# Two attention blocks in fp32 on one core: VectorE items between PSUM reads, the place of the first scores, and statistics on ScalarE

## The chip, the cores and the metric

The kernel runs on one core of a Trainium2 chip. The metric is the device time in microseconds of one execution; before the change it is 3248.27 us (median of 3 runs, 3246.43 to 3249.09). The profile is of one execution of its own, with a span of 3242.0 us, and all times inside the kernel below are microseconds from the start of that span.

A core has five engines that run side by side, each through its own list of instructions: TensorE (PE in the profile; its weight loads are PEld) multiplies matrices and writes to PSUM, VectorE (DVE) and ScalarE (ACT) work elementwise and read PSUM, GpSimd (POOL) and SyncE (SP) here mostly start transfers (DMA).

## The reference

Two attention blocks follow each other on an input of 8 images, 512 channels and 32 x 32 = 1024 positions. Both compute the same thing with weights of their own (biases and the affine part of the norm are applied too):

```python
def block(x):                                  # x: (8, 512, 1024)
    xg = x.reshape(8, 8, -1)                   # group norm, 8 groups of 64 channels
    xn = (xg - xg.mean(-1)) * rsqrt(xg.var(-1) + 1e-5)
    q, k, v = wq @ xn, wk @ xn, wv @ xn        # 512 x 512 each, 8 heads of 64
    p = softmax(q.T @ k * 64 ** -0.5, -1)      # per head, 1024 x 1024
    return x + wp @ (p @ v) + bias
return block1(block0(x))
```

All of it is fp32. The kernel works through 16 jobs, (image, block) pairs, two images in turn: (0, 0), (1, 0), (0, 1), (1, 1), (2, 0) and so on.

## The kernel before

Each job is a norm, three projections, an attention and an output projection. The projections use Strassen-like products: a 512 x 512 product becomes 7 products of halves; those for v stay at that level (the *v phase*), and those for the output (O), for k and for q are split once more into 7 *inner products* each. One stage of the kernel therefore does 21 *chains* of 7 inner products: O of the job before, then K and Q of the next. With the 64 steps of an attention a job has three stages:

- v phase, 7 products in two halves, while the output sums of the job before are formed
- the 21 chains (`deep_phases`; 14 in the first, where there is no O)
- attention: 8 groups (pair of heads, half of the positions) of 8 steps; a step makes scores on TensorE, their exp on ScalarE, a running sum on VectorE, and two steps later the value product on TensorE

A chain keeps its partial sums in four PSUM banks. Seven products go through three or four of them in the order 1, 5, 6, 2, 7, 3, 4, and each result is read by ScalarE (`copy`, `put(.., 0, ..)`) or by VectorE (`put(.., 1, ..)`, which adds `s5`):

```python
ORDER = (1, 5, 6, 2, 7, 3, 4)
def step(o):
    product(o, {1: z, 5: w, 6: z, 2: y, 7: z, 3: u, 4: z}[o], o in (1, 5))
    if o == 1:   nc.scalar.copy(y, z)
    elif o == 5: put5(w)             # ScalarE: s5 <- w
    elif o == 6: nc.scalar.copy(u, z)
    elif o == 2: put(0, 0, y)        # ScalarE
    elif o == 7: put(1, 1, z)        # VectorE reads z ...
    elif o == 3: put(0, 1, u)        # VectorE
    else:        put(1, 0, z)        # ... which o == 4 has written again; ScalarE
```

Two chains are interleaved, on the two halves of PSUM. VectorE has other work in this stage, which waits in three queues and is put into its instruction list just after its two PSUM reads in a chain: `soon` (sums that the next chains need: the `deep` sums of xn and the output sums of the chain after next), `outer` (the second level of the Strassen sums, 1024 elements each, and the additions to x) and `extra` (the statistics of the next norm, among others):

```python
def thunk(c, j):
    def go():
        if j == 0:
            live[c] = begin(c)           # may put four items into soon
        live[c](ORDER[j])
        if ORDER[j] in (7, 3):
            if soon:
                soon.popleft()()
            if outer:
                outer.popleft()()
            elif extra and extra[0][0] <= c:
                extra.popleft()[1]()
        if j == 6:
            end(c)                       # puts one to three items into outer
        ...
at = sorted((7 * c + 2 * j, c, j) for c in range(len(chains)) for j in range(7))
return [thunk(c, j) for _, c, j in at]
```

`begin` also forms the weight sums of the chain after next with four small VectorE additions (`factor`) where these weights are used for the first time: K and Q of block 0 ahead of the first attention, O of block 0 after it, K and Q of block 1 in the next stage, O of block 1 in the one after; later jobs load the finished sums. Four of the seven results of an output chain are added to x by an accumulating DMA on the GpSimd queue, started in `end`, and the others by VectorE.

At the end of the stage half 0 of PSUM is given to the scores while the last chain, on half 1, still has products to do; then half 1 is given to the value products:

```python
both = deep_phases(n + 1, extra, outs, ...)
both[0]()
rest[0]()
if n < 0:
    later(12.0, lambda: load_x(1))       # the second image, 2 MB
for thunk in both[1:-3]:
    thunk()
banks(0, "two")
att = Attention(n + 1)
att.scores(0)
att.scores(1)
for thunk in both[-3:]:
    thunk()
banks(1, "two")
```

`later(us, fn)` puts an instruction into its list after so many microseconds of a count of the products already listed; it waits for nothing at run time. The tile of the second image holds raw weights of q until they are stored, so that `load_x(1)` can start only after that.

The statistics of a norm are taken on VectorE, two half rows and an aggregation for each of four chunks of 128 channels. A gather through DRAM by two DMAs then brings them to eight partitions (`gather`), `groups` forms mean and variance, and `factors` and `apply` (ScalarE, four passes of 1024 elements) make xn:

```python
def stat(self, cc, sh):
    nc.vector.bn_stats(self.stats[:, cc, sh, :], xs[self.b][:, cc, sh * HALF : (sh + 1) * HALF])
    if sh == 1:
        nc.vector.bn_aggr(self.mv[:, cc, :], ...)
...
reads = [lambda cc=cc, sh=sh: norm.stat(cc, sh) for cc in range(NC) for sh in range(2)]
reads.append(norm.gather)
steps = [norm.groups, factors] + [lambda cc=cc: norm.apply(cc) for cc in range(NC)]
```

What is left of `extra` is put into the attention from step 2 on, one item a step, and `steps` and the sums of xn at fixed steps (10, 19, 22, 24, 26, 28, 36, 39, 42, 45). In the first attention the eight statistics of the second image come there, beside the weight sums of later jobs (`first_factors`), which the attentions of jobs 0 to 2 have.

Of the kernel before, what the change touches and what calls it, by code (L numbers as in the profile page):

```python
# [9 lines left out]
F32 = mybir.dt.float32  # L10
I32 = mybir.dt.int32
AF = mybir.ActivationFunctionType
ALU = mybir.AluOpType
# [5 lines left out]
P = 128  # L19
B, C, H, W = 8, 512, 32, 32  # L20
S = H * W
# [5 lines left out]
NC = C // P  # L27
# [43 lines left out]
def fast_path(  # L71
# [10 lines left out]
    nc = tc.nc  # L82
    xpool = ctx.enter_context(tc.tile_pool(name="xpool", bufs=2))
    acts = ctx.enter_context(tc.tile_pool(name="acts", bufs=1))
# [17 lines left out]
    xs = {}  # L102
# [3 lines left out]
    def later(delay, fn):  # L106
        todo.append((clock[0] + delay, fn))
# [34 lines left out]
    factors, deep = {}, {}  # L142
# [6 lines left out]
    def factor(w, part):  # L149

        if part == 0:
            nc.vector.tensor_add(w[:, S1], w[:, S3], w[:, A22])
        elif part == 1:
            nc.vector.tensor_sub(w[:, S2], w[:, S1], w[:, A11])
        elif part == 2:
            nc.vector.tensor_sub(w[:, S3], w[:, A11], w[:, S3])
        else:
            nc.vector.tensor_sub(w[:, S4], w[:, A12], w[:, S2])
# [53 lines left out]
    def load_x(b):  # L212
        for cc in range(NC):
            nc.sync.dma_start(xs[b][:, cc, :], x[b, cc * P : (cc + 1) * P, :])

    class Norm:
# [11 lines left out]
        def stat(self, cc, sh):  # L228
# [3 lines left out]
            if sh == 1:  # L232
                nc.vector.bn_aggr(
                    self.mv[:, cc, :], self.stats[:, cc, :, :].rearrange("p s k -> p (s k)")
                )

        def gather(self):

            dm = dram.tile([2, NC, HD, 2], F32, tag="dm", name=f"dm_{self.n}")
            for h in range(2):  # L240
                nc.sync.dma_start(
                    dm[h].rearrange("c p k -> p c k"), self.mv[h * HD : (h + 1) * HD]
                )
            self.gm = small.tile([GROUPS, HD, 2], F32, tag="gm", name=f"gm_{self.n}", bufs=1)
            nc.sync.dma_start(self.gm, dm.rearrange("h c p k -> (h c) p k"))
# [62 lines left out]
    def norm_steps(n):  # L308
        norm = Norm(n)

        def factors():
            norm.factors(slice(0, NC))
            xn[0] = acts.tile([P, NC, S], F32, tag="xn", name=f"xn_{n}")

        reads = [lambda cc=cc, sh=sh: norm.stat(cc, sh) for cc in range(NC) for sh in range(2)]
        reads.append(norm.gather)
        steps = [norm.groups, factors] + [lambda cc=cc: norm.apply(cc) for cc in range(NC)]
        return reads, steps

    xn, tx, to = [None], [None], [None]  # L320
# [182 lines left out]
    def deep_phases(n, extra, outs=None, early=()):  # L503
# [160 lines left out]
# [3 lines that stand above are left out]
                    live[c] = begin(c)  # L667
                live[c](ORDER[j])
                if ORDER[j] in (7, 3):
                    if soon:  # L670
                        soon.popleft()()
                    if outer:
                        outer.popleft()()
                    elif extra and extra[0][0] <= c:
                        extra.popleft()[1]()
                if j == 6:
                    end(c)
                    if c + 1 == len(chains):
                        while outer:
                            outer.popleft()()  # L680
                advance(0.43)

            return go
# [194 lines left out]
    def sums(n):  # L878


        def start():
            tx[0] = acts.tile([P, 3, 2, HALF], F32, tag="t", name=f"t_{n}")
            combine(xn[0], tx[0], 0)

        return [start] + [lambda part=part: combine(xn[0], tx[0], part) for part in (1, 2, 3)]
# [137 lines left out]
    def normed(chunks, cols):  # L1023
        for cc in chunks:
            norm.apply(cc, cols, cc % 2 == 1)
# [7 lines left out]
    var()  # L1033
    for i in range(3):
        idle_products(i % 2, "y", f"again_b{i}")
    for sh in range(2):
        norm.stat(2, sh)
    norm.factors(slice(0, 2))
    normed((0, 1), left)
    normed((0, 1), right_)  # L1040
    factor(v0, 0)
    for sh in range(2):
        norm.stat(3, sh)
# [46 lines left out]
    extra.append((6, load))  # L1090
    extra.extend((9, fn) for fn in bias_steps)
    reads, steps = norm_steps(1)
    extra.extend((10, fn) for fn in reads)
    for n in range(-1, len(jobs)):
        last = n + 1 == len(jobs)
        outs = None
        if n >= 0:
            chores = {}

            def put(i, fn):  # L1100
                while i in chores:
                    i += 1
                chores[i] = fn

            if last:
                w = plain_weights(n)
            else:
                if n == 0:
                    first_factors(put, [(O, 0), (V, 1)])
                elif n == 1:  # L1110
                    first_factors(put, [(K, 1), (Q, 1)])
                elif n == 2:
                    first_factors(put, [(O, 1)])
                for i, (_, fn) in enumerate(extra):
                    put(2 + i, fn)
                at = (10, 19, 22, 24, 26, 28, 36, 39, 42, 45)
                for i, fn in zip(at, steps + sums(n + 1)):
                    put(i, fn)
                deep_first = deep_steps(n + 1)
                for at, fn in zip((52, 54, 57, 59), deep_first[4:]):  # L1120
                    put(at, fn)
                put(61, lambda: (extend_plan(n + 1), [fetch() for _ in range(RING)]))
            assert max(chores, default=0) < NT * len(att.groups)
            att.run(chores)
            banks(0, "one")
            banks(1, "one")
            if last:
                advance(100.0)
                advance(100.0)
                judge()  # L1130
                plain_proj(n, w)
                break
            outs = OutputSums(n)
            out_sums(n, outs)
            first = v_phase(n + 1, ORDER)
            for thunk in first[:-1]:
                thunk()
            rest = first[-1:]
            extra = deque()
            if jobs[n][1] == 1 and jobs[n][0] + 2 < B:  # L1140
                extra.append((11, lambda b=jobs[n][0] + 2: (x_tile(b), load_x(b))))
            if n == 1:
                load, bias_steps = make_out_bias(1)
                extra.append((8, load))
                extra.extend((11, fn) for fn in bias_steps)
            if n + 2 < len(jobs):
                reads, steps = norm_steps(n + 2)
                extra.extend((15, fn) for fn in reads)
        both = deep_phases(n + 1, extra, outs, deep_first[:4] if outs else ())
        both[0]()  # L1150
        rest[0]()
        if n < 0:
            later(12.0, lambda: load_x(1))
        for thunk in both[1:-3]:
            thunk()
        banks(0, "two")
        att = Attention(n + 1)
        att.scores(0)
        att.scores(1)
        for thunk in both[-3:]:  # L1160
            thunk()
        banks(1, "two")

# [248 lines left out]
```

## Time and profile before

| | |
|---|---|
| time, median of 3 | 3248.27 us |
| span of the profile | 3242.0 us |
| TensorE busy | 3203.7 us |
| VectorE busy | 2771.0 us |
| ScalarE busy | 1896.9 us |
| mean DMA rate | 97 GB/s |
| granted clock of TensorE | 1.0 throughout |

The profile's first part gives each engine's busy time. The list of waits names for each engine and line what ended its idle time before an instruction, with the total, the number of times and the longest, in microseconds. The timeline lists instructions with start, duration, engine, line of the kernel, operation, output and input, and in brackets the idle time ahead of it and what ended it. An fp32 matmul of the inner products shows as two passes (x2); its duration includes the pipeline, so that the distance of two starts, not the duration, is what one costs. Matmul lines: L565 inner products, L434 products of the v phase, L736 scores, L767 values. PSUM reads by VectorE in the chains: L579 and L581; by ScalarE: L575, L577 and the copies at L381, L385 and L583. L594 are `outer` sums, L610 additions to x, L463 to L468 output sums, L366 to L372 `deep` sums, L152 to L158 weight sums, L229 and L233 statistics, L277 the applications of the norm, L753 the running sums of the attention and L783 their reduction.

### The profile page before, as it was taken

The page shows a single profiled execution, that of the slowest core. Times are in us where ns is not written, and L with a number is a line of the kernel's source. Part 1 is how long each engine was busy: PE and PEld are TensorE (multiplying, and loading weights), DVE is VectorE, ACT ScalarE, POOL GpSimd, SP SyncE. Part 2 cuts the span into 40 slices and gives each one's busy share as a digit, 9 for nine tenths or more (in the row PEclk, how much of TensorE's full clock was granted, in tenths as well). Part 3 has the DMA queues.
Part 4 walks back from the last instruction along what each step waited for, and adds up shares of the span by engine and source line. Part 5 has one row for each costly group of instructions (what it writes and reads, how often), then busy time and mean ns, then how long its engine had stood idle before and what let it go on. Part 6 is the DMA issues. An engine that isn't in the chain of part 4 may idle for free.

```text
span 3242.0 us, 57681 instructions
## 1 busy us (share of the span) xinstructions
PE 3203.7 (99%) x22870; PEld 1846.3 (57%) x22870; DVE 2771.0 (85%) x3968; ACT 1896.9 (59%) x3022; POOL 98.9 (3%) x93
## 2 busy tenths in 40 slices
PE   9999999999999999999999999999999999999999
PEld 7356384563836638366483654737547374573743
DVE  8997998979889797897978879788897888978876
ACT  4646646466564665656656565565656656566463
POOL 0000000000000000000000000000000000000000
PEclk9999999999999999999999999999999999999999
DMA  8234162350613305034160421505216051140501
GB/s 313 96 100 132 67 206 68 94 170 22 207 28 84 93 25 158 22 103 126 33 205 19 112 72 37 146 15 139 96 44 191 16 141 43 55 129 22 168 25 41
DMA packets 149462, 313.04 MB, mean 97 GB/s; under 512 B 33864, under 2 KB 46784, under 8 KB 148160
## 3 DMA queue, kind: packets, MB, share of 16 engines
q1 hardware_dynamic: 132320, 276.77, 26.0%
q0 software_dynamic: 16864, 32.51, 6.2%
q8 instruction: 181, 2.97, 0.4%
q14 instruction: 97, 0.79, 0.1%
HBM read 224.35 MB, written 51.18 MB: 85 GB/s over the span
## 4 chain that ended last, share of the span: by engine, by line
PE 89%; DVE 8%; DMA 1%; issue 1%; ACT 0%; DVEq 0%; SPq 0%
PE sc L736 26%; PE po L767 26%; PE vd L565 10%; PE zd L565 9%; PE z L434 6%; PE yd L565 4%; PE ud L565 3%; PE v L434 1%; PE u L434 1%; PE y L434 1%; DVE acc L753 1%; PE pp L705 1%; DVE p L581 1%; DVE x L610 1%; DVE p L594 1%
## 5 line engine op out<-in xcount | busy, mean ns | idle before, releaser
L741 ACT ACTIVATE e<-sc 128x1024 f32<-128x1024 f32 x1024 | 1046.8, 1024 | 584.9 <-PE sc L736 499.3
L736 PE MATMUL sc<-q,k 64*64 64x512 f32 x8192 | 1061.9, 590 | 2.0
L767 PE MATMUL po<-e,v 64*64 64x512 f32 x8192 | 1057.4, 589 | 0.0
L753 DVE TENSOR_TENSOR acc<-acc,e 128x1024 f32<-128x1024 f32 x768 | 935.9, 1219 | 54.8 <-ACT e L741 6.6
L767 PEld LDWEIGHTS po<-e,v 64*64 64x64 f32 x8192 | 313.2, 133 | 565.8 <-issue 556.7
L736 PEld LDWEIGHTS sc<-q,k 64*64 64x64 f32 x8192 | 310.0, 133 | 561.9 <-issue 545.7
L565 PE MATMUL vd<-deep,w 128*128 128x256 f32 x900 | 256.3, 383 | 5.1 <-DVE p L581 4.9
L565 PE MATMUL zd<-deep,w 128*128 128x256 f32 x892 | 248.1, 380 | 3.8 <-DVE p L579 3.2
L751 DVE TENSOR_TENSOR acc<-e,e 128x1024 f32<-128x1024 f32 x128 | 156.3, 1221 | 100.1 <-ACT e L741 100.1
L565 PEld LDWEIGHTS vd<-deep,w 128*128 128x128 f32 x900 | 167.9, 190 | 48.2 <-DVE p L581 13.0
L565 PEld LDWEIGHTS zd<-deep,w 128*128 128x128 f32 x892 | 169.0, 190 | 29.0 <-DVE p L579 5.1
L783 DVE TRANSPOSE_TENSOR_REDUCE r<-acc 128x32 f32<-128x1024 f32 x128 | 158.5, 1239 | 0.6
L565 PE MATMUL vd<-os,w 128*128 128x256 f32 x420 | 122.1, 384 | 14.5 <-DVE p L579 12.6
L608 POOL DMA_DIRECT2D x<-p x62 | 74.6, 1203 | 1996.8 <-ACT p L575 1521.9
L594 DVE TENSOR_TENSOR p<-p,p 128x1024 f32<-128x1024 f32 x94 | 114.2, 1215 | 0.0
L434 PE MATMUL z<-w,t 128*128 128x256 f32 x480 | 110.9, 379 | 0.0
L434 PE MATMUL z<-w,xn 128*128 128x256 f32 x480 | 110.1, 382 | 0.0
L385 ACT COPY ud<-vd 128x256 f32<-128x256 f32 x173 | 61.8, 357 | 77.2 <-PE vd L565 63.8
L583 ACT COPY s<-zd 128x256 f32<-128x256 f32 x173 | 64.5, 373 | 71.5 <-PE zd L565 71.5
L447 ACT COPY v<-z 128x512 f32<-128x512 f32 x32 | 18.8, 586 | 148.7 <-PE z L434 148.7
L434 PEld LDWEIGHTS z<-w,xn 128*128 128x128 f32 x480 | 90.0, 190 | 23.8 <-issue 12.2
L385 ACT COPY ud<-zd 128x256 f32<-128x256 f32 x156 | 55.7, 357 | 76.5 <-PE zd L565 74.6
(207 smaller groups left out, 4049.3 us busy)
## 6 DMA issues: line engine op xcount, KB each, us to landing
w<-deep SPq DMA_DIRECT2D x287, 448.0 KB, 3.9
w<-keep SPq DMA_DIRECT2D x129, 256.0 KB, 2.7
x<-p POOLq DMA_DIRECT2D x62, 512.0 KB, 6.9
rb<-rd SPq DMA_DIRECT2D x96, 256.0 KB, 4.0
deep<-w SPq DMA_DIRECT2D x42, 448.0 KB, 3.6
x<-x_dram SPq DMA_DIRECT2D x28, 512.0 KB, 6.4
out_dram<-x SPq DMA_DIRECT2D x28, 512.0 KB, 6.0
keep<-raw SPq DMA_DIRECT2D x5, 1792.0 KB, 7.7
```

Of the source, the lines that this page charges most:

```text
L385: nc.scalar.copy(u, z)
L434: nc.tensor.matmul(ps[:, ti * CH : (ti + 1) * CH], r[:, cc, t0 : t0 + P], w[:, cc, :], start=(start and ti == 0 and cc == 0), stop=(cc == ...
L565: nc.tensor.matmul(ps, lhs[:, FACTOR[i], :], moving[i], start=start, stop=True, skip_group_check=True,)
L583: return chain(product, lambda ps: nc.scalar.copy(s5, ps), put, z, y, u, w)
L594: outer.append(lambda: nc.vector.tensor_add(to_, a, b))
L608: nc.gpsimd.dma_start(to_, p(part), accum_op=ALU.add)
L736: nc.tensor.matmul(sc[h * HD : (h + 1) * HD, j, :], k[r, hp, k0 : k0 + HD], q[r, hp, sh * HALF : (sh + 1) * HALF], start=True, stop=True,)
L741: nc.scalar.activation(e, sc, AF.Exp, scale=SCALE)
L751: nc.vector.tensor_add(acc[g], self.es[i - 1], e)
L753: nc.vector.tensor_add(acc[g], acc[g], e)
L767: nc.tensor.matmul(po[g][j * HD : (j + 1) * HD, h, :], v[r, kc, d0 : d0 + HD], e[r, j, :], start=(kc == 0), stop=(kc == NT - 1),)
L783: nc.vector.tensor_reduce(self.r[:, 0, m, :], self.acc.pop(g).rearrange("p j (b e) -> p (j b) e", e=RP), AX.X, ALU.add, apply_transpose=True,)
```

## The change

It has five parts.

1. In a chain, one item at most goes onto VectorE's list after a PSUM read: an `outer` item only where no `soon` item was put.
2. The scores of the next attention are put two inner products from the end of q, no longer three.
3. The statistics of the second image (job 1) are taken by ScalarE in the first attention, as sums of x and then of (x - mean)^2 by the accumulator of an activation, whose elementwise output goes to the xn tile, which is free then. They no longer stand in `extra`; the later steps of that norm and the sums of xn move to later steps of the attention.
4. The load of the second image comes at 22 in place of 12.
5. At the start, the second half of one statistic of the first image moves behind the first applications of the norm.

Parts 1 and 2 are meant to keep VectorE's reads from standing behind other work while TensorE needs the bank, part 3 to take work off VectorE in an attention where it has the most, and part 4 to let weight loads go ahead of x.

```diff
+        def sums(self, cc):
+            nc.scalar.activation(
+                xn[0][:, cc, :], xs[self.b][:, cc, :], AF.Identity, accum_out=self.mv[:, cc, 0:1]
+            )
+        def less_mean(self):
+            nc.vector.tensor_scalar(self.off, self.mv[:, :, 0], -1.0 / S, None, ALU.mult)
+        def squares(self, cc):
+            nc.scalar.activation(
+                xn[0][:, cc, :], xs[self.b][:, cc, :], AF.Square, bias=self.off[:, cc : cc + 1],
+                accum_out=self.mv[:, cc, 1:2],
+            )
+        def by_count(self):
+            nc.vector.tensor_scalar(self.mv, self.mv, 1.0 / S, None, ALU.mult)
 ...  # norm_steps
+        if n == 1:
+            reads = [place] + [lambda cc=cc: norm.sums(cc) for cc in range(NC)]
+            reads.append(norm.less_mean)
+            reads += [lambda cc=cc: norm.squares(cc) for cc in range(NC)]
+            reads.append(lambda: (norm.by_count(), norm.gather()))
+            return reads, [norm.groups, factors] + [...]
 ...  # thunk of deep_phases
                     if soon:
                         soon.popleft()()
-                    if outer:
+                    elif outer:
                         outer.popleft()()
 ...  # start
-    for sh in range(2):
-        norm.stat(2, sh)
+    norm.stat(2, 0)
     norm.factors(slice(0, 2))
     normed((0, 1), left)
     normed((0, 1), right_)
+    norm.stat(2, 1)
 ...
     reads, steps = norm_steps(1)
-    extra.extend((10, fn) for fn in reads)
 ...  # ahead of each attention
                 at = (10, 19, 22, 24, 26, 28, 36, 39, 42, 45)
+                if n == 0:
+                    for i, fn in zip((3, 3, 4, 5, 6, 8, 10, 11, 12, 13, 15), reads):
+                        put(i, fn)
+                    at = (22, 30, 34, 35, 37, 38, 41, 44, 47, 50)
 ...
         if n < 0:
-            later(12.0, lambda: load_x(1))
-        for thunk in both[1:-3]:
+            later(22.0, lambda: load_x(1))
+        for thunk in both[1:-2]:
             thunk()
 ...
-        for thunk in both[-3:]:
+        for thunk in both[-2:]:
             thunk()
```

More of the change, by code (lines that the diff above doesn't have):

```diff
@@ L309, in norm_steps, with place @@
         norm = Norm(n)
+        def place():
+            xn[0] = acts.tile([P, NC, S], F32, tag="xn", name=f"xn_{n}")
         def factors():
             norm.factors(slice(0, NC))
-            xn[0] = acts.tile([P, NC, S], F32, tag="xn", name=f"xn_{n}")
+            if n > 1:
+                place()
+        if n == 1:
[3 more added lines that the diff above has]
+            reads.append(lambda: (norm.by_count(), norm.gather()))
+            return reads, [norm.groups, factors] + [lambda cc=cc: norm.apply(cc) for cc in range(NC)]
         reads = [lambda cc=cc, sh=sh: norm.stat(cc, sh) for cc in range(NC) for sh in range(2)]
```

## The prediction

> **What bounds the kernel now.** I read the shares of busy time first, then TensorE's waits, then the order of time around each wait.
>
> ```profile
> span 3242.0 us, 57681 instructions
> PE 3203.7 (99%) x22870; PEld 1846.3 (57%) x22870; DVE 2771.0 (85%) x3968; ACT 1896.9 (59%) x3022; POOL 98.9 (3%) x93
> ...
> PE vd L565 <- DVE p L579: 12.6, 15, 1.6
> PE vd L565 <- DVE p L581: 6.7, 22, 0.7
> PE zd L565 <- DVE p L579: 4.5, 4, 2.9
> PE v L434 <- DVE q L790: 2.5, 1, 2.5
> ...
> PEld sc L736 <- ACT p L577: 8.0, 15, 0.5
> ```
>
> The page says TensorE (PE) is busy for 99% and VectorE (DVE) for 85%: TensorE bounds the kernel, and no change that leaves its matmuls alone can gain more than its gaps. The waits (total us, times, longest) say where the gaps are: nearly all are matmuls of the inner products (L565) that wait for a VectorE read of the PSUM bank they are to overwrite (L579 and L581), once in each of the 15 later jobs at vd, and once at the scores. One wait of 2.5 us stands alone (L434), as does one of 2.9 us.
>
> The scores of successive jobs start, by the chain in order of time, at 83.59, 289.94, 495.90, 698.17 and 898.05 us and then every 199.88 us: the first three jobs take 206.35, 205.96 and 202.27 us, the other twelve 199.88. I laid the TensorE timeline of one such period against its own cadence (two passes of 128x256 in 0.43 us, a score or value step in 0.86) and got about 2 us that do no work, in two places. The first, from the timeline of all engines in job 3 after its start at 898 us:
>
> ```profile
> 1047.54 1.22 DVE L594 TENSOR_TENSOR p<-p,p 128x1024 f32<-128x1024 f32 x1
> ...
> 1049.40 0.41 DVE L468 TENSOR_TENSOR os<-to,os 128x256 f32<-128x256 f32 x1
> 1049.74 1.22 DVE L610 TENSOR_TENSOR x<-x,p 128x1024 f32<-128x1024 f32 x1
> 1050.03 0.59 PE L565 MATMUL vd<-os,w 128*128 128x256 f32 x2
> 1050.87 0.41 DVE L579 TENSOR_TENSOR p<-vd,s 128x256 f32<-128x256 f32 x1
> 1051.34 0.70 PE L565 MATMUL vd<-os,w 128*128 128x256 f32 x2 [0.71 <-DVE p L579]
> ```
>
> The columns are start, duration, engine, line, operation. Between two PSUM reads VectorE had both an item of `soon` (L467/L468) and one of `outer` (L610); so the read (L579) started at 1050.87, and the matmul that reuses the bank at 1051.34, where the cadence put it at 1050.46: 0.88 us lost. The second place, where the scores are put in:
>
> ```profile
> 1097.40 0.47 ACT L577 ACTIVATE p<-zd,bias_step 128x256 f32<-128x256 f32 x1
> 1097.93 1.95 PE L736 MATMUL sc<-q,k 64*64 64x512 f32 x16
> 1099.81 0.70 PE L565 MATMUL vd<-deep,w 128*128 128x256 f32 x2
> 1100.34 0.59 PE L565 MATMUL ud<-t,w 128*128 128x256 f32 x2
> 1100.61 0.48 DVE L581 SCALAR_TENSOR_TENSOR p<-vd,vec_sb,s 128x256 f32<-128x256 f32 x1 [1.80 <-PE vd L565]
> 1101.15 0.30 PEld L565 LDWEIGHTS vd<-deep,w 128*128 128x128 f32 x2 [0.61 <-DVE p L581]
> 1101.78 0.21 PEld L736 LDWEIGHTS sc<-q,k 64*64 64x64 f32 x8 [0.33 <-issue]
> ```
>
> The product before the scores ended at 1097.63; they waited 0.30 us for ScalarE to empty a bank of half 0. After them come the last three products: vd (o=7), ud (o=3), vd (o=4). The last overwrites what VectorE reads from the first, so it came at 1101.15 instead of 1100.77: 0.38 us. The remaining 0.45 us are the changes between 64-row and 128-row matmuls (0.15 and 0.20, and a slower first product), which stay.
>
> **What the Trainium skill says.** "PSUM — Partial Sum Buffer", section "Engine vs sequencer instructions", says that ScalarE, VectorE and GpSimdE queues are strict FIFO; the lines above agree: the 0.41 us read stood behind the 1.22 us addition. The same page, section "PSUM bank collisions raise a hardware error", wants semaphores by bank between a reader and TensorE, which is the wait here. "ScalarE: Activation LUTs", section "Table sets: the hidden batching unit", says that cheap functions are in every set and that a switch of sets costs a load; the profile shows one load (1283 ns) for Identity and Exp together, and the built program of the changed kernel also has one, so I take it that Square brings none. "DMA: Bandwidth & Descriptors", section "Issuing engines are not separate DMA queues", says that all transfers share 16 engines; in the first 90 us they are busy nearly throughout at a mean 292 GB/s, so a moved 2 MB load matters there.
>
> **The change part by part.** *One item per read (`elif`).* With one item of 1.13 us (its spacing in the run of adds) and two reads of 0.34 to 0.40 us, VectorE needs about 2 x (1.13 + 0.40) = 3.06 us for an inner chain of 7 x 0.43 = 3.02 us on TensorE: just even. With two items in a slot (0.77 + 1.13) it needs some 4.6 us in chain 3, which is the lag seen. After the change the `soon` items run in chains 0 to 3 and the six or seven `outer` items one by one in chains 5 to 8. I went through the order of the built program: the additions to x at L610 still stand ahead of the DMA accumulations to the same quarters (o=3 and o=4), so VectorE isn't made to wait for a DMA of 6.9 us. Gain: 12 jobs x 0.88 = 10.6 us; in jobs 0, 1 and 2 the corresponding gap is 1.33, 1.81 and 1.33, of which I give 4.0, since job 1 still has its weight sums between (0.93 us a chain). Together 14.6. Their earlier gaps (0.79 and 0.80 in jobs 0 and 2) come from the weight sums beside the `deep` sums and stay.
>
> *Two products from the end.* The o=7 product goes ahead of the scores: they start 0.43 us later than 1097.63, at 1098.06, when the bank (read until 1097.87) is free; and VectorE reads o=7 during the 1.72 us of scores. Gain 0.30 + 0.38 = 0.68 in 15 jobs and 0.38 in the first (no wait at 83.59): 10.6 us. The next step needs half 1 free: ScalarE would end its last read behind two exps at about 1101.6, and the value products come at about 1101.95, so I expect no new wait, by a margin of 0.3 us.
>
> *Statistics by ScalarE.* In the first attention VectorE loses 8 x 0.68 + 4 x 0.21 = 6.2 us and gets two small ones (0.3). It ends that attention behind: its last reduction (L783) starts at 201.99 where TensorE had done the last values at 195.87. That is the 2.5 us wait at L434 (2.71 with its restart) and some 0.35 at 227.87. The idle 3.59 us before the group statistics (they were asked for before their DMA had landed) also goes, as they stand at step 22. Gain 3.0. ScalarE takes on 8 passes from SBUF: an existing one (L277, 128x1024) takes 1.23 us, against an exp's 1.02. Four stand in successive steps: about 0.93 + 1.14 (each less the 0.09 by which two in a row overlap, as two exps take 1.94) and a read of the accumulator, an estimated 0.1 to 0.2, in a step of 1.716, so the lag grows 0.36 to 0.55 a step, 1.4 to 2.2 us in four; the score buffers allow some 1.3. I take 0.7 us off for this and the four applications in a row later. Net 2.3.
>
> *x load at 22 instead of 12.* At 67.35 a product waits 2.89 us (3.05 with restart) for VectorE, which waited for weights whose DMA was issued at 58.09, behind the 2 MB load of x, and landed after 7.82 us where the median of such loads in the first 90 us is 4.1. Now the load comes after three more weight loads; only the weights of the last chain are behind it. Gain 3.05 - 0.5 for those = 2.5.
>
> *Half a statistic moved at the start.* The first application starts some 0.5 us earlier, but TensorE then waits for the statistics of the last chunk all the same (pm at 14.50). 0.
>
> Sum: 14.6 + 10.6 + 2.3 + 2.5 + 0 = 30.0 us, or 0.9%; 3248.3 - 30.0 = 3218.3.
>
> **Rivals.** *VectorE becomes the bound*: the additions put off pile up in front of K's own and the statistics from chain 15. For it: 3.06 against 3.02 us. Against it: VectorE idles 0.4 to 1.7 us at nearly every read from 1059 to 1066, and has 13 us free of 61 in this stage. If true, half of 14.6 comes back: about 3226. *The scores' gaps return as a wait of the value products for half 1*: the margin is 0.3 us; it would give back up to 0.5 in each of 16, about 3226. *ScalarE's lag holds the scores up in the first attention*: four late buffers in place of one wait; up to 3 us, so part three nets nothing: 3221. *All is hidden behind TensorE*: not possible for these, as each gap is in TensorE's own timeline.
>
> **Range and chances.** The two large terms are counted from repeated gaps; each could be a quarter too large (6 us), the two small ones could be nothing (5 us). Little can make it better: jobs 0 to 2 have perhaps 4 us more. I set 3219.5, from 3213 to 3230. Over 2% would need 65 us, more than all gaps of TensorE together (38.3 us outside its busy time), so chance 0.01; over 2% slower needs a serious new wait, 0.01.
>
> **What would show it.** In the profile after, the wait of vd for L579's successor should fall from 12.6 to under 3 us, that of the scores for ScalarE from 8.0 to near the plain restart, and the period from 199.88 to about 198.3. The wait at L434 and the 2.89 us wait should be gone; ScalarE's busy time in the first attention should rise by some 10 us. A wait of x additions for a DMA, of value products for L577's successor or of scores for exps in the first attention would make me wrong.

## The result and the profile after

The changed kernel takes 3216.26 us (median of six runs, 3215.33 to 3217.55) where the kernel before takes 3247.69 (six runs beside them, 3246.43 to 3249.09). The ratio is 0.9904, with a 95% interval from 0.9891 to 0.9916. The span of the profile goes from 3242.0 to 3213.6 us, 28.4 less.

The medians thus differ by 31.4 us, 3 more than the profiles. The profile of before is of an execution of 3243.87 us, shorter than all six above, with a granted clock of 1.0 up to its last 2 us. The profiles of the first two runs below, which keep the long waits near 67 and 205 us (2.2 to 3.3 us), show TensorE at half clock just after them: for 6.8 and 3.4 us in one, for 3.4 and 3.4 in the other. The profiled execution of before has these waits without such a stretch. The changed kernel and its variants have no gap of 2 us or more, and no such stretch before their last 4 us. So some of the 3 us may come from these waits too; no run tests it.

In the changed kernel the lines of code stand lower: the inner products are L593 (before L565), VectorE's reads of them L607 and L609 (L579, L581), the scores L764 (L736), the products of the v phase L462 (L434), the additions to x L638 (L610), the running sums of the attention L779 and L781 (L751, L753) and their reduction L811 (L783). New are ScalarE's sums, L239, and squares, L247. The page begins like this, and TensorE's waits after it (total us, times, longest) answer to those shown of before:

```profile
span 3213.6 us, 57636 instructions
PE 3194.8 (99%) x22870; PEld 1850.2 (58%) x22870; DVE 2767.3 (86%) x3958; ACT 1902.4 (59%) x3038; POOL 99.4 (3%) x93
...
PE zd L593 <- DVE p L607: 3.3, 4, 1.4
PE vd L593 <- DVE p L609: 2.9, 6, 0.6
PE zd L593 <- DVE p L609: 1.9, 3, 0.9
PE pm L311 <- DVE mv L233: 1.8, 2, 1.2
...
PE v L462 <- DVE q L818: 1.3, 1, 1.3
...
PEld sc L764 <- ACT p L605: 5.2, 16, 0.3
```

The 12.6 us of vd on the first read are gone from the list, those on the second are 2.9 where they were 6.7, and the scores wait 16 times for 0.33 at most, the plain restart after ScalarE. What is left is in single places: the v phase (1.3, before 2.5) and a few waits of zd. The scores of successive jobs, by the chain in order of time:

| us | first scores | job 0 | job 1 | job 2 | jobs 3 to 14, each | last scores to end |
|---|---|---|---|---|---|---|
| before | 83.59 | 206.35 | 205.96 | 202.27 | 199.88 | 145.24 |
| after | 82.67 | 204.53 | 203.02 | 200.51 | 198.21 | 144.33 |
| difference | -0.92 | -1.82 | -2.94 | -1.76 | 12 x -1.67 = -20.0 | -0.91 |

The two places of a steady period that the prediction took apart look like this in the timeline of the changed kernel (start, duration, engine, line). First VectorE at the place where an item of `soon` and one of `outer` had stood together; the period starts at 888.94:

```profile
1037.84 0.41 DVE L495 TENSOR_TENSOR os<-to 128x256 f32<-128x256 f32 x1
...
1038.18 0.42 DVE L496 TENSOR_TENSOR os<-to,os 128x256 f32<-128x256 f32 x1
...
1039.28 0.42 DVE L607 TENSOR_TENSOR p<-vd,s 128x256 f32<-128x256 f32 x1 [0.68 <-PE vd L593]
...
1039.62 1.21 DVE L622 TENSOR_TENSOR p<-p,p 128x1024 f32<-128x1024 f32 x1
...
1039.94 1.03 PE L593 MATMUL vd<-os,w 128*128 128x256 f32 x4
```

Only the item of `soon` (L495 and L496) stands ahead of the read, so VectorE waits for TensorE there and no longer the reverse. The last line is two products in a row; the second writes the bank that the read at 1039.28 has emptied, with no idle time ahead of it. Then the scores, now with two products after them:

```profile
1086.56 0.59 PE L593 MATMUL vd<-deep,w 128*128 128x256 f32 x2
...
1087.08 1.95 PE L764 MATMUL sc<-q,k 64*64 64x512 f32 x16
...
1087.66 0.48 DVE L609 SCALAR_TENSOR_TENSOR p<-vd,vec_sb,s 128x256 f32<-128x256 f32 x1
...
1088.96 0.70 PE L593 MATMUL ud<-t,w 128*128 128x256 f32 x2
...
1089.50 0.59 PE L593 MATMUL vd<-deep,w 128*128 128x256 f32 x2
...
1090.13 0.47 ACT L605 ACTIVATE p<-vd,vec_sb 128x256 f32<-128x256 f32 x1
...
1090.93 1.04 PE L795 MATMUL po<-e,v 64*64 64x512 f32 x8
```

VectorE reads o=7 (1087.66) while the scores run, so the last vd comes 0.54 us after ud with nothing named ahead of it. ScalarE's last read of half 1 ends at 1090.60, and the value products come at 1090.93: the margin of 0.3 us that the prediction gave was there.

### The profile page after: what moved, and what is told of

The parts are those of the page before. It is cut to its first block, busy times and chain, and to the rows that moved or that the text cites. A ratio compares the mean times of both kernels' runs of the same rounds, so it can differ in the third digit from the quotient of the medians.

```text
span 3213.6 us, 57636 instructions
## 1 busy us (share of the span) xinstructions
PE 3194.8 (99%) x22870; PEld 1850.2 (58%) x22870; DVE 2767.3 (86%) x3958; ACT 1902.4 (59%) x3038; POOL 99.4 (3%) x93
## 4 chain that ended last, share of the span: by engine, by line
PE 93%; DVE 5%; DMA 1%; issue 1%; ACT 0%; SPq 0%; POOL 0%; DVEq 0%
PE sc L764 27%; PE po L795 26%; PE vd L593 10%; PE zd L593 10%; PE z L462 6%; PE ud L593 4%; PE yd L593 4%; PE v L462 2%; PE y L462 2%; PE u L462 2%; DVE acc L781 1%; PE pp L733 1%; DMA x<-p 0%; DMA w<-wqkv_dram 0%; DVE w L154 0%
## 5 line engine op out<-in xcount | busy, mean ns | idle before, releaser
L764 PE MATMUL sc<-q,k 64*64 64x512 f32 x8192 | 1061.7, 590 | 0.0
L781 DVE TENSOR_TENSOR acc<-acc,e 128x1024 f32<-128x1024 f32 x768 | 936.3, 1219 | 57.8 <-ACT e L769 9.3
L764 PEld LDWEIGHTS sc<-q,k 64*64 64x64 f32 x8192 | 309.7, 133 | 559.1 <-issue 545.4
L593 PE MATMUL vd<-deep,w 128*128 128x256 f32 x900 | 252.6, 380 | 1.4 <-DVE p L609 1.3
L779 DVE TENSOR_TENSOR acc<-e,e 128x1024 f32<-128x1024 f32 x128 | 156.4, 1222 | 111.3 <-ACT e L769 111.3
L593 PE MATMUL zd<-deep,w 128*128 128x256 f32 x892 | 248.4, 380 | 3.7 <-DVE p L607 2.0
L593 PEld LDWEIGHTS vd<-deep,w 128*128 128x128 f32 x900 | 170.6, 190 | 26.4 <-DVE p L609 2.5
L593 PEld LDWEIGHTS zd<-deep,w 128*128 128x128 f32 x892 | 168.9, 190 | 29.2 <-DVE p L607 3.3
L811 DVE TRANSPOSE_TENSOR_REDUCE r<-acc 128x32 f32<-128x1024 f32 x128 | 158.5, 1238 | 0.5
L593 PE MATMUL vd<-os,w 128*128 128x256 f32 x420 | 118.1, 380 | 1.6 <-DVE p L609 1.5
L462 PE MATMUL z<-w,t 128*128 128x256 f32 x480 | 110.9, 379 | 0.0
L462 PE MATMUL z<-w,xn 128*128 128x256 f32 x480 | 110.1, 382 | 0.0
L462 PEld LDWEIGHTS z<-w,xn 128*128 128x128 f32 x480 | 90.0, 190 | 23.8 <-issue 12.2
```

The source lines that it names most:

```text
L462: nc.tensor.matmul(ps[:, ti * CH : (ti + 1) * CH], r[:, cc, t0 : t0 + P], w[:, cc, :], start=(start and ti == 0 and cc == 0), stop=(cc == ...
L593: nc.tensor.matmul(ps, lhs[:, FACTOR[i], :], moving[i], start=start, stop=True, skip_group_check=True,)
L764: nc.tensor.matmul(sc[h * HD : (h + 1) * HD, j, :], k[r, hp, k0 : k0 + HD], q[r, hp, sh * HALF : (sh + 1) * HALF], start=True, stop=True,)
L779: nc.vector.tensor_add(acc[g], self.es[i - 1], e)
L781: nc.vector.tensor_add(acc[g], acc[g], e)
L811: nc.vector.tensor_reduce(self.r[:, 0, m, :], self.acc.pop(g).rearrange("p j (b e) -> p (j b) e", e=RP), AX.X, ALU.add, apply_transpose=True,)
```

## The experiments

In what the experiments expect, Theory 1 and Theory 2 are those that each text states. Where one time is given without a ratio, the kernel was executed once with its profile; what is concluded rests on places in the profile, not on the time.

### One item per read, alone

The kernel before, with part 1 only:

```diff
-                    if outer:
+                    elif outer:
```

> The kernel before with the one-item rule alone (an outer item only where no soon item was put). My account (a VectorE read that stood behind two items): in jobs 3 to 14 the period of the scores falls from 199.88 by 0.88 to 199.00 us, the 0.30 and 0.38 us gaps at the scores stay, and the wait of vd for the read at L579 (12.6 us) falls below 3 us; span about 3242 - 13 = 3229, ratio about 0.996. Rival (the work put off makes VectorE the bound later): the period falls by less than half of that and new waits for VectorE appear between chains 7 and 15.

Measured: 3233.5 us, ratio 0.9954 (0.9938 to 0.9971). The twelve steady periods are 198.90, which is 0.98 less each. Of TensorE's waits:

```profile
PE zd L565 <- DVE p L579: 6.7, 5, 3.3
PE vd L565 <- DVE p L581: 6.3, 22, 0.6
PE v L434 <- DVE q L790: 2.5, 1, 2.5
```

The line of vd on L579 (12.6) has gone, and the one on L581, which is the place of the scores, stays with its 22 times. So part 1 does what it was meant to, at 0.98 a job where 0.88 had been counted from one gap. The other tenth is in the product after the wait. In the kernel before it starts at 1051.34 and the next at

```profile
1051.87 0.59 PE L565 MATMUL yd<-q,w 128*128 128x256 f32 x2
```

which is 0.53 us later, where products otherwise follow in 0.43. The line of zd grew from 4.5 to 6.7; half of that is a wait in job 0 that went from 0.34 to 1.45 us (see "One addition of the first job on VectorE").

### The scores two products from the end, alone

The kernel before, with part 2 only:

```diff
-        for thunk in both[1:-3]:
+        for thunk in both[1:-2]:
 ...
-        for thunk in both[-3:]:
+        for thunk in both[-2:]:
```

> The kernel before with the first scores two inner products from the end instead of three, and nothing else. My account (the scores wait for ScalarE to empty half 0, the last product for VectorE's read of the third last): the period of jobs 3 to 14 falls by 0.68 to 0.8 us to about 199.1, the wait at 1050 of 0.71 us stays in every job; span about 3242 - 11 = 3231, ratio about 0.997. Rival (the gap moves to the value products, which then wait for half 1): a period of 199.4 or more and waits of the value products for ScalarE's read in each job.

Measured: 3237.28 us, ratio 0.9968 (0.9958 to 0.9979), steady periods 199.20, which is 0.68 less.

```profile
PE vd L565 <- DVE p L579: 12.6, 15, 1.6
...
PE vd L565 <- DVE p L581: 3.3, 6, 0.7
```

The mirror image: the wait on L579 stays whole, and the one on L581 loses 16 of its 22 times. 0.98 + 0.68 = 1.66, and both together gave 1.67. The two parts take away separate gaps, and neither gives back anything of the other.

### One product after the scores in place of two

```diff
-        for thunk in both[1:-2]:
+        for thunk in both[1:-1]:
 ...
-        for thunk in both[-2:]:
+        for thunk in both[-1:]:
```

> The changed kernel with the first scores one inner product from the end in place of two. My account of part two (three left: a wait for ScalarE's half 0 and one for VectorE's read; two left: neither; the margin of the value products against ScalarE's read of half 1 is about 0.3 us): with one left the scores still don't wait, but ScalarE's last read comes after both exps and the value products follow one product less after the scores, so they wait about 0.1 to 0.2 us: period of jobs 3 to 14 198.3 to 198.4 in place of 198.21. Rival (the further from the end the scores, the more is lost, as they only interrupt the products): the period falls below 198.15.

Measured: 3215.55 us, steady periods 198.21 as in the changed kernel. The small loss that was expected didn't come. One product or two after the scores makes no difference here; in both kernels the matmul of o=7 comes ahead of them.

### The second input's statistics back on VectorE

The changed kernel, with the statistics as VectorE items in `extra` again, but with the later steps (22, 30, 34 ...) of part 3 kept:

```diff
-        if n == 1:
+        if False:                       # the statistics by ScalarE are not used
 ...
+    extra.extend((10, fn) for fn in reads)
 ...
-                    for i, fn in zip((3, 3, 4, 5, 6, 8, 10, 11, 12, 13, 15), reads):
-                        put(i, fn)
```

> The changed kernel with the second image's statistics back on VectorE, but with the group statistics and what follows them at the later steps of the changed kernel. Theory 1 (in the first attention VectorE was late because it idled 3.59 us for the gather of the statistics; the later steps cure that, and the ScalarE passes cost VectorE 5.3 us of waiting for exps): VectorE idles under 2 us between steps 2 and 62, its last reduction starts 3 us or less after TensorE's last value product, against 4.3 in the changed kernel, and the wait of the v phase for VectorE (1.26 us) is gone; the first job's period falls from 204.52 to about 203.1. Theory 2 (taking 6.2 us of work off VectorE is what helped): the last reduction starts about 6 us late, the wait in the v phase is 2.5 us again, and the period is about 205.8.

Measured: 3216.28 us; the gap in the v phase is 0.80, smaller than the 1.42 of the changed kernel (1.20 in its second profile), and the first period is 203.49 in place of 204.53. Taking the statistics off VectorE gave nothing; the later steps alone give more. Why is seen in what VectorE waited for in the first attention (84 to 200 us), in the changed kernel:

```profile
DVE acc L781 <- ACT e L769: 2.9, 6, 0.8
DVE acc L779 <- ACT e L769: 2.4, 2, 1.6
DVE lt L842 <- DMA r<-r: 2.1, 1, 2.1
```

and in this one, with the statistics on VectorE:

```profile
DVE acc L778 <- ACT e L768: 1.0, 1, 1.0
DVE acc L780 <- DVE acc L780: 0.5, 1, 0.5
DVE acc L780 <- DVE acc L778: 0.5, 1, 0.5
```

ScalarE's eight passes stand between the exps, but delay them little: the ninth exp ends 16.35 us after the first scores where it is 15.42 with the statistics on VectorE, which is the largest delay, and from the seventeenth on they are level. VectorE, freed of the statistics, has nothing to do and waits for exps (5.3 us in all), and once for a transfer. Up to its last reduction it is busy for 102.07 us (106.53 before) and waits for 7.4 (3.6 before): most of what it was relieved of became idle time at a place where it keeps up with the exps. The kernel before had one such wait there, of 3.6 us for the transfer ahead of the group statistics, and the later steps remove it without help from ScalarE.

### ScalarE's passes spread out

The changed kernel with the passes at wider steps:

```diff
-                    for i, fn in zip((3, 3, 4, 5, 6, 8, 10, 11, 12, 13, 15), reads):
+                    for i, fn in zip((3, 3, 5, 7, 9, 11, 11, 13, 15, 17, 20), reads):
 ...
-                    at = (22, 30, 34, 35, 37, 38, 41, 44, 47, 50)
+                    at = (26, 32, 34, 35, 37, 38, 41, 44, 47, 50)
```

> The changed kernel with ScalarE's eight passes over the second image spread over steps 4 to 20 (at most two in a row) instead of 4 to 14, and the group statistics four steps later. Theory 1 (exps that come late behind passes in successive steps starve VectorE, which can't make up for it): VectorE's waits for exps in the first attention fall from 5.3 us to under 2.5, the wait for the gathered row sums of 2.1 us goes as its DMA is no longer behind the statistics', the last reduction starts 1 to 2 us after TensorE's last value product, and the v phase doesn't wait; first period about 203.1. Theory 2 (VectorE's lag comes from the work of the later steps, the sums of xn and the deep sums, alone): the last reduction starts some 4 us late as before and the period stays at 204.5.

Measured: 3217.24 us; gap in the v phase 1.95, first period 205.51. VectorE's waits for exps stayed at 5.2 us (the two lines of L779 and L781), and a wait of 2.1 us for a transfer (rb, at 132.65) took the place of the one at 122.77. The expectation of my own theory fell: spreading didn't take the waits away, which fits idle time better than late exps.

### VectorE's weight sums earlier

The changed kernel with the eight weight sums of the first attention at steps 9 to 22 in place of 12 to 33, so that they fill the idle time:

```diff
-                at += 3
+                at = next(places) if early else at + 3      # 9, 12, 15, 17, 19, 20, 21, 22
```

> The changed kernel with the eight weight sums of the first attention at steps 9 to 22 in place of 12 to 33, so that three of them leave the stretch after step 22; no work is added or taken away. Theory 1 (VectorE catches up and idles up to about step 19, 7.8 us in all, so work taken off it there is lost, and only what stands later counts): its waits in the first attention fall from 7.8 to about 4 to 5 us, the last reduction starts about 2 us less late (some 3 in place of 4.84 us after TensorE's last value product), the wait of the v phase for VectorE falls from 1.26 to 0 or nearly, and the first period from 204.53 to 203.1 to 203.5. Theory 2 (only the total of VectorE's work in the attention counts): the last reduction stays 4.8 us late and the first period at 204.5.

Measured: 3215.61 us; gap in the v phase 1.79, first period 205.15. The wait at 122.77 shrank to 0.3, as it should, but another took its place twelve microseconds later:

```profile
134.47 1.23 DVE L872 TENSOR_TENSOR q<-q,rb 128x1024 f32<-128x1024 f32 x1 [2.20 <-DMA rb<-rd]
```

So this expectation fell too: VectorE's idle time moved, and did not shrink.

### Half of the weight sums on GpSimd

Two more runs were to tell whether only VectorE's work after its last idle time counts. GpSimd does four of the eight weight sums, either the first four or the last four:

```diff
-                put(at, lambda i=i, part=part: factor(box[0][:, i], part))
+                put(at, lambda ...: factor(box[0][:, i], part,
+                    nc.gpsimd if <first attention> and i == 0 else None))    # the other run: i == 1
```

> The changed kernel with four of the eight weight sums that VectorE does beside the first attention (its steps 12 to 21, 0.68 us each, at 106.7 to 125.6 us, that is before or at VectorE's last idle time at 122.8) put on GpSimd. Theory 1 (what decides the wait at the layer's end is only the work that VectorE gets after its last idle time in the attention): these four take the place of idle time, so VectorE's idle time there grows by about 2 to 2.7 us, its last reduction still ends near 4.8 us behind TensorE's last value product, the wait of the value projection stays near 1.3 us and the period from the first scores to the second stays near 204.5. Theory 2 (the total of VectorE's work beside the attention decides): the reduction comes 2.7 us nearer to the value product, the wait falls below 0.5 us and the period to about 203.1. If GpSimd's sums slow VectorE's own instructions, it shows in the length of VectorE's additions of that stretch (0.4 to 1.2 us each before).

> The same with the other four sums (steps 24 to 33, at 129.4 to about 146 us, after VectorE's last idle time at 122.8). Theory 1: four times 0.68 = 2.7 us less lag at the end (about 2.1 us where it was 4.84), the wait of the value projection (1.3 us) all but gone, first period near 203.1; unless VectorE catches up in that stretch and finds a new wait, in which case its last idle time moves later and the lag falls by less than 2.7 by just that idle time. Theory 2: the same figures as with the early four, since the total is the same.

Measured: 3216.53 and 3214.21 us; first periods 203.94 and 202.85; gap in the v phase 0.46 in both. The pair doesn't tell the theories apart, as no step held GpSimd back: it did its sums between 92 and 103 us in both runs, and VectorE grew slow there. GpSimd and then VectorE in the run with the last four, from the timeline:

```profile
97.97 2.26 POOL L157 TENSOR_TENSOR raw<-raw 128x512 f32<-128x512 f32 x1
100.18 2.34 POOL L159 TENSOR_TENSOR raw<-raw 128x512 f32<-128x512 f32 x1
...
94.77 4.33 DVE L782 TENSOR_TENSOR acc<-acc,e 128x1024 f32<-128x1024 f32 x2 [0.44 <-ACT e L770]
99.02 1.24 DVE L245 TENSOR_SCALAR off<-mv 128x4 f32<-128x4 f32 x1
```

Two additions took 4.33 us, where two in a row otherwise take 2.54, and a four-element operation 1.24, which takes 0.17 in the changed kernel. The Trainium skill, "SBUF — State Buffer", section "Who interferes with whom", says that a VectorE instruction with two inputs in SBUF contends with a GpSimd instruction that reads SBUF, for a pair of ports that one of them holds exclusively. The additions agree with it: each grew by 0.9 us, beside GpSimd sums that took 1.27 us (the first) to 2.34. The four-element operation has one input, so that this sentence does not cover it; it grew by 1.07. So the pair took 2.7 us of work off VectorE and made its other work longer in an earlier stretch.

Against Theory 1, the early four helped as much as the late four. Against Theory 2, the lag did not fall by 2.7 us. What the pair does show is a floor. Let the lag be the time from TensorE's last value product, by its cadence, to the start of VectorE's last reduction:

| kernel | VectorE's last idle time in the first attention | lag | gap of TensorE in the v phase |
|---|---|---|---|
| before | 116.1 | 6.12 | 2.71 |
| passes spread out | 132.7 | 5.36 | 1.95 |
| weight sums earlier | 142.4 | 5.19 | 1.79 |
| changed kernel | 122.8 | 4.84 | 1.42 |
| changed kernel, second profile | 122.8 | 4.62 | 1.20 |
| statistics on VectorE, later steps | 167.9 | 4.21 | 0.80 |
| GpSimd, first four | 155.4 | 3.88 | 0.46 |
| GpSimd, last four | 154.5 | 3.87 | 0.46 |
| best (below) | 153.2 | 3.88 | 0.46 |

The gap is the lag less 3.41 in every row, to 0.01. So the wait follows from VectorE's lag alone in nine profiles. Where VectorE comes to wait for an exp once more at about 153 to 156, it has caught up, and the work placed after that leaves a lag of 3.9 (or 4.2). Where it does not, backlog remains at the end, and its size isn't told by the last idle time alone: the second to fourth rows are not in order.

### The start

The changed kernel with the old order of the first statistics (part 5 undone) and the second image's load still later:

```diff
-    norm.stat(2, 0)
+    for sh in range(2):
+        norm.stat(2, sh)
 ...
-    norm.stat(2, 1)
 ...
-            later(22.0, lambda: load_x(1))
+            later(27.0, lambda: load_x(1))
```

> The changed kernel with the statistics at the start in the old order and the second image's load at 27 in place of 22. My account: the old order takes 0.6 us off the start (the mean product of the last chunk waits 0.5 us for VectorE as before the change, not 1.20, and starts near 14.5), and with the weights of the last chain issued ahead of x the wait of 0.93 us (1.10 with restart) at 75.07 goes, so that the first scores come at about 81.0 us in place of 82.67, if the first loads of the input land alike. Rival for the load (x now comes too late for ScalarE's first sums, at step 4): the first scores still come at 81 to 81.5, but ScalarE waits for x at about 89 us and the first period grows by the wait. Rival for the start (the first landing of the input decides): no difference in the wait of the mean product.

Measured: 3213.95 us; first scores at 81.44, 1.23 earlier. In the changed kernel the weights of the last chain stand behind the 2 MB load of x (issued at 64.95 and 62.21), as the prediction had it, and VectorE waits for them:

```profile
73.60 0.29 DVE L152 TENSOR_TENSOR w<-w 128x128 f32<-128x128 f32 x1 [1.24 <-DMA w<-wqkv_dram]
...
75.07 0.70 PE L593 MATMUL zd<-deep,w 128*128 128x256 f32 x2 [0.93 <-DVE p L609]
```

With the load at 27 that gap of TensorE (1.10 us with its restart) is gone, and the later x holds nothing up. In nine profiles with the load at 22 the gap is 1.08 to 1.92, and in the two with it at 27 there is none. On part 5 the run gave no answer, since VectorE waited 0.37 us for the first weights. Over all runs, the gap of pm near 15 us is 1.28 to 1.39 in the nine profiles with the new order, and 0.76, 0.76, 0.98, 1.20 and 1.23 in the five with the old. The new order gains nothing and probably costs up to 0.6; how much isn't settled.

### One addition of the first job on VectorE

In job 0 the changed kernel has a gap of 1.53 us that was 0.49 before. Its cause by the timeline:

```profile
247.76 1.22 DVE L638 TENSOR_TENSOR x<-x,p 128x1024 f32<-128x1024 f32 x1 [2.25 <-DMA x<-p]
...
248.91 0.42 DVE L607 TENSOR_TENSOR p<-zd,s 128x256 f32<-128x256 f32 x1
...
249.38 0.70 PE L593 MATMUL zd<-deep,w 128*128 128x256 f32 x2 [1.36 <-DVE p L607]
```

VectorE's addition to x waits for an accumulating DMA to the same quarter (10.98 us from its issue, by the chain); the read stands behind the addition, and TensorE behind the read. In this run VectorE makes that addition too, in the first output only:

```diff
-                    more(1, 1, 5, m in (0, 2))
+                    more(1, 1, 5, m == 2)       # m == 0: an addition on VectorE, no DMA
```

> The changed kernel with one addition to x in job 0 (product 5 to the fourth quarter) on VectorE in place of an accumulating DMA. My account (VectorE's next addition to the same quarter waits for that DMA, 2.25 us of idle at 247.8 with a load and a landing of 11 us, and the PSUM read behind it holds TensorE 1.36 us): that wait and the gap of 1.53 us at 249.4 go, VectorE gets one more item of 1.13 us in chain 5 to 8 at no cost, and the first period falls from 204.53 to 203.0. Rival (VectorE has no room in this stage, as it forms the weight sums of O there): the gap stays in another place and the period is 204.0 or more.

Measured: 3213.93 us; first period 202.85, which is 1.68 less, and the gap is gone. The cause is shown.

The kernel before had the same wait, behind a transfer of 9.29 us, at a cost of 0.49 us to TensorE:

```profile
250.41 1.23 DVE L610 TENSOR_TENSOR x<-x,p 128x1024 f32<-128x1024 f32 x1 [2.09 <-DMA x<-p]
```

In the profiles of the kernels with part 1 that make this transfer, it takes 10.26 to 11.68 us; without part 1, 9.23 and 9.29. Why it grew isn't shown.

### What the runs point to, together

```diff
+ statistics on VectorE, with the later steps kept
+ old order at the start, load of the second image at 27
+ the addition of job 0 on VectorE
```

> The changed kernel with what the earlier runs pointed to: the statistics of the second input on VectorE again but with the later steps kept, the last addition of the first job at the outer place on VectorE (no wait for a transfer that adds), the old order at the start and the load of the first input's second half at step 27. From the single edits: 2.2 us less (start with the load), 1.7 less in the first job, and 1.0 less for the value projection's wait where statistics stay on VectorE: sum 4.9, less what they share; I expect first scores at 81.5 to 82.2, first period 201.8 to 202.6, the rest as in the changed kernel, and 3211.5 to 3213.5 us against 3216.3. A rival: VectorE, with the addition of job 0 and the statistics on it as well, runs out of slack in the first job and the gain of the edits doesn't add up, 3214 to 3216.

> The changed kernel once more, to be timed beside the next one: 3216.3 us, ratio 0.990.

Measured on one chip, in turn: 3212.13 us (3211.45 to 3212.85), the changed kernel 3215.92 (3214.71 to 3217.26), the kernel before 3247.89. The ratios to before are 0.9888 (0.9872 to 0.9905) and 0.9899 (0.9882 to 0.9915). The ranges of the two new ones don't touch: 3.8 us less. The first scores come at 81.07, the first period is 202.54. In the first attention VectorE waits 1.3 us for exps, and for no transfer:

```profile
DVE acc L778 <- ACT e L768: 1.3, 2, 1.0
DVE p L608 <- PE ud L592: 0.4, 1, 0.4
```

Of the five parts this version keeps the first two, the later steps of part 3, and part 4 with a later place.

## Why the prediction was right, step by step

The time predicted was 3219.5 us, from 3213 to 3230; it is 3216.26. By the profile's span, term by term:

| term | predicted | measured | from |
|---|---|---|---|
| one item per read | 10.6 + 4.0 = 14.6 | 11.8 + 4.2 - 1.0 = 15.0 | 12 x 0.98 of the run alone; rest of jobs 0 to 2; the wait for a DMA |
| two products from the end | 10.6 | 10.7 | 15 x 0.68 + 0.91 at the end - 0.43 at the start |
| statistics by ScalarE, later steps | 2.3 | 1.3 | gap in the v phase 2.71 to 1.42 |
| load of x at 22, order of the start | 2.5 + 0 | 1.35 | 3.05 gone, 1.10 new, 0.60 more at pm |
| sum | 30.0 | 28.4 | |

The 4.2 is what is left of 6.52 in jobs 0 to 2 after 3 x 0.68 and 1.29, with the 1.04 by which the gap of job 0 grew put back. By their own times the first two parts alone gave 13.1 us (9.4 to 20.1) and 9.4 (6.8 to 13.6), too wide to check the terms by; the terms rest on the periods.

**One item per read** was right in its mechanism and close in size: the count from one gap was 0.10 a job short, for the slower product after the wait. The step that failed is "VectorE isn't made to wait for a DMA of 6.9 us": it held in the steady jobs, but in job 0 VectorE waits 2.25 us for a transfer of 10.98. The trace of before had the wait already (2.09 us), and 6.9 is the median of all 62 such transfers. It was called a thing that would make the prediction wrong; it cost 1.0 us. A smaller gap of job 0, where zd waits for ScalarE's copy of yd (0.47, and 1.06 in the best version), is not in before and was not followed up.

**Two products from the end** was right to 0.1 us, and the first value products came with the margin given. The 0.68 itself is partly luck: of the 0.30 at the scores only 0.20 went, as 0.09 of the change to the scores' tiles stays (1086.56 to 1087.08 is 0.52), and the 0.38 ahead of the last product was 0.48 with the slower product after it.

**Statistics by ScalarE** gave 1.3 us where 2.3 was counted, and for another reason; that it came so near is luck. The step that failed is that VectorE's 6.2 us less of work would end the wait at L434. VectorE was busy for 4.5 us less up to its last reduction, but waited 3.8 us more, and the wait at L434 stayed at 1.3 us. In the 112.3 us from the first scores ScalarE's busy time rose by 7.7 us (73.69 to 81.39; some 10 predicted). ScalarE's lag, put at 1.4 to 2.2 us in four steps, was 0.9, and the 0.7 taken off for it was not needed: TensorE had no gap in the first attention. The gain is that of the later steps, as the run with the statistics back on VectorE shows.

**The load** lost its 3.05 as said, but "0.5 for those" behind it was 1.10. **The order of the start** was put at 0, and TensorE's gap there grew by 0.60 in this profile.

**The rivals.** VectorE did not become the bound, and the value products didn't wait. Of the third, scores held up by ScalarE, there was a lag of 0.9 us, and no score waited for it.

## What to carry to other kernels

Where a queue runs in order and a bottleneck engine waits for its reads, count what can stand between two reads in the worst slot, not the engine's share of busy time: a one-word change in that slot was worth some 15 us here by the periods, and taking the statistics off the same engine nothing. Before moving work off an engine, ask whether it is behind at that place: where VectorE kept up with the exps, relief became idle time. Look in the first repetitions for transfers slower than in the steady ones, and for waits on them that the trace of before has already.

## What was not expected of the hardware

- A pass of ScalarE over 128x1024 from SBUF with an accumulator takes 1.06 us (Identity) or 1.14 (Square with a bias), and the accumulator's read is an instruction of its own, 0.20 and 0.19 us.
- GpSimd's first addition of 128x512 took 1.27 us and the next ones 2.1 to 2.3, beside a VectorE at work; VectorE takes 0.68 for the same. In the run with the first four sums, four additions of VectorE to its running sum took 8.81 us in that stretch (2.2 each, where they otherwise follow each other in 1.33). Small sums on GpSimd are not free for VectorE.
- Accumulating transfers of the same kind and size took 5.1 to 9.9 us after 900 us in the changed kernel, and one in its first job 10.98.
